# Two cross-attention layers: the order of the context loads, and the sources of one sum of adding transfers

## The chip, the core and the metric

The kernel runs on one core of one Trainium2 chip. The metric is the time of one execution in microseconds (us), as the device counts it; a kernel's time is the median of several executions. A profile is one more execution, and has its own time.

The engines are named as in the profile: PE is TensorE's matrix multiplication and PEld its loading of weights, DVE is VectorE, ACT ScalarE, POOL GpSimd, SP SyncE. SP computes nothing here; it issues transfers. A transfer is issued on the queue of the engine whose program holds it, and is carried by the core's 16 DMA engines.

## What is computed

Two layers of cross-attention over the same context `ctx` (8 batches of 1444 keys of width 512), for 8 batches of 100 queries of width 1024; all is float32. The reference, cut to what matters:

```python
def layer0(query, key):
    Q = query @ Wq + bq
    K = key @ Wk + bk
    V = key @ Wv + bv
    weights = softmax(Q @ K.T / sqrt(1024), axis=-1)
    return query + (weights @ V) @ Wo + bo

def layer1(emb, latent):
    q = emb @ Wq + bq
    k = latent @ Wk + bk
    v = latent @ Wv + bv
    w = softmax(q @ k.T / sqrt(1024), axis=-1)     # over the keys
    x = w @ v + emb
    return layernorm(x) * gamma + beta             # eps 1e-6

out = layer1(layer0(x, ctx), ctx)
```

## The kernel before

Keys and values are never formed. The kernel multiplies the weights first: `qk` is Wq Wk^T and `vo` is Wv Wo, so that the scores are (x `qk`) ctx^T and the result is (weights ctx) `vo`. All the large products of weights and of queries use a scheme with seven half products in place of eight (`weight_products`, L348; `queries`, L653; `inner_product`, L256). The stages follow each other on TensorE in the program's order, which is kept by hand for that engine (`manual_schedule(engines={PE})`, L64):

1. `qk` of layer 0, then `vo`, then the queries of layer 0, then `qk` of layer 1 (call at L846);
2. the scores of batches 0 and 1 of layer 0 (L1296 and L1299);
3. a loop over the eight batches (L1300). In each, `alternated` (L1284) interleaves the weighted rows of batch b (`weighted_rows`, L883) with the scores of batch b + 2 (`scores_by_keys`, L922), step by step. In the first turn the first 12 steps of the scores go ahead;
4. the output projection and the queries of layer 1, and then the same for layer 1.

**The context is loaded twice for each batch and layer.** `load_features` (L855) loads the transposed context ctx^T as four feature tiles of 128 rows by 1444, two transfers each; the scores of a batch go through them in order, 46 records of TensorE a tile (23 matrix multiplications, each of which the profile shows as two). `load_rows` (L864) loads the context itself as four row tiles of three blocks of 128 keys, one transfer a block; the last tile has two blocks and a remainder in two transfers. In this document cT_b_k is feature tile k of batch b and c_b_q is row tile q.

**Where the tiles lie.** Row tiles, and the feature tiles 0 and 1, take a buffer of the pool `unit` (L72), of which there are ten; the units of `qk`, eight of them, come from the same pool, as do some temporaries. The feature tiles 2 and 3 take a buffer with the tag `prob` (`feature_block`, L84), of which there are three: prob0, prob1 and prob2. A load into a buffer waits until all that used it before is done.

**What sets the order.** Outside TensorE a scheduler places each instruction on its engine when the kernel is built; where it holds that a buffer comes free late, it puts other instructions first. `tc.keep_in_program_order(instruction)` takes an instruction out of this freedom against others of its kind on the same engine. An engine executes its list in order, and an instruction that waits holds up those behind it; this is true of SP's list of loads too.

**The bias sums.** Four sums over the eight units of a weight product, each unit scaled by one bias per row, are made beside the products. Those of width 1024 go through `transferred_sum` (L547). It scales a unit into a tile on ScalarE (`scaled_sum`, L576; activations at L579, in program order), and then adds the tiles in pairs, as a tree, with adding transfers issued by GpSimd (`transfer_added`, L573; the transfers are at L574): tile 0 takes tile 1, tile 2 takes 3, 4 takes 5, 6 takes 7; then 0 takes 2 and 4 takes 6; then 0 takes 4. For `qk` of layer 1 all eight tiles are scaled at once. Its tiles are, by number: two rows, one weight row, prob0, prob1, prob2, and two weight rows. The same three prob buffers carry, just before, part of the key bias of layer 0 (`key_bias_sums`, L624, call at L844), which ends in a transfer that adds prob0 to the tile `kb`; and just after, the feature tiles 2 and 3.

The finished sum is read by VectorE in `block_sums` (L586; the transpose at L592 and the reduction at L595), after the softmax of batch 0 (call at L1298). ScalarE also copies finished half products out of PSUM (`put`, L436 to L438), between and behind the scalings; TensorE accumulates further on such a bank only after its copy.

As built, SP's loads after those of the weights were not in the program's order: batch 0 in order, then the first half of cT_1_2, then cT_1_0, the second half of cT_1_2, cT_1_1, then the row tiles of batch 0 mixed with the first feature tiles of batch 2, and cT_1_3 after all of c_0.

Of the kernel before, what the change touches and what calls it, by code (L numbers as in the profile page):

```python
# [31 lines left out]
P = 128  # L32
HP = P // 2
B, T, E = 8, 100, 1024
S, L = 1444, 512
# [11 lines left out]
LAST = (MC - 1) * P  # L47
PAD = S - LAST + QD
# [5 lines left out]
def two_layer_cross_attention(ctx: ExitStack, tc: tile.TileContext, a: dict, out: bass.AP):  # L54
    nc = tc.nc
# [16 lines left out]
    def unit(name):  # L72
        return stream.tile([P, E + L], F32, tag="unit", name=name)

    def wide(name):
        return work.tile([P, LC, GT], F32, tag="AT", name=name, bufs=2)

    def row(name):
        return work.tile([P, E], F32, tag="row", name=name, bufs=3)

    def weight_rows(name):
        return work.tile([P, MC * T], F32, tag="wT", name=name, bufs=3)

    def feature_block(name):  # L84
        return work.tile([P, S], F32, tag="prob", name=name, bufs=3)
# [262 lines left out]
    def weight_products(name, left, right, l_width, r_width, scaled, between=None):  # L348
# [35 lines left out]
        def accumulate(side):  # L384
            for v, of in scaled:
                if of != side:
                    continue
                width = (l_width, r_width)[side]
                first = 0 if side == 0 else l_width
                srcs = [(units[h][:, first : first + width], cols[v][:, h : h + 1]) for h in range(EC)]  # L390
                if width == E:
                    accs[v] = transferred_sum(f"{name}_{v}", srcs, name)
                    continue
                acc = work.tile([P, L], F32, tag="half", name=f"{name}_{v}", bufs=1)
                accs[v] = acc
                if early:
                    tiles = [acc] + [t[:, i * L : (i + 1) * L] for t in prob for i in range(2)]
                    scaled_sum(tiles + [weight_rows(f"{name}_{v}_7")[:, :L]], srcs)
                    continue
                for h, (src, by) in enumerate(srcs):  # L400
                    if h == 0:
                        vector.tensor_scalar(acc, src, by, None, ALU.mult)
                    else:
                        vector.scalar_tensor_tensor(acc, src, by, acc, ALU.mult, ALU.add)
# [142 lines left out]
    def transferred_sum(name, srcs, of):  # L547

        n = EC if of == "qk1" else EC // 2
        tiles = [row(f"{name}_{n}") for n in range(2)] + [weight_rows(f"{name}_2")[:, :E]]
        tiles += [t[:, :E] for t in prob]
        if of != "qk0":
            tiles += [weight_rows(f"{name}_{n}")[:, :E] for n in range(6, 8)]
        scaled_sum(tiles[:n], srcs[:n])

        def second_half():
            t = tiles[n]  # L560
            if of != "qk0":
                scaled_sum(tiles[n:], srcs[n:])
            else:
                for i, (src, by) in enumerate(srcs[n:]):
                    if i == 0:
                        vector.tensor_scalar(t, src, by, None, ALU.mult)
                    else:
                        vector.scalar_tensor_tensor(t, src, by, t, ALU.mult, ALU.add)
            transfer_added(tiles[0], t)

        return tiles[0], second_half

    def transfer_added(to, t):  # L573
        nc.gpsimd.dma_start(out=to, in_=t, accum_op=ALU.add)  # L574

    def scaled_sum(tiles, srcs):  # L576

        for t, (src, by) in zip(tiles, srcs):
            tc.keep_in_program_order(nc.scalar.activation(t, src, AF.Copy, scale=by))  # L579
        k = 1  # L580
        while k < len(tiles):
            for i in range(0, len(tiles) - k, 2 * k):
                transfer_added(tiles[i], tiles[i + k])
            k *= 2
# [39 lines left out]
    def key_bias_sums(name, wqbk, tiles=()):  # L624

        acc = to = work.tile([P, B * T], F32, tag="kb", name=name, bufs=1)

        def steps():
            if tiles:
                scaled_sum(tiles, [(xT[:, k, :], wqbk[:, k : k + 1]) for k in range(EC)])
            for k in range(len(tiles), EC):
                if k == len(tiles):
                    vector.tensor_scalar(to, xT[:, k, :], wqbk[:, k : k + 1], None, ALU.mult)
                else:
                    vector.scalar_tensor_tensor(to, xT[:, k, :], wqbk[:, k : k + 1], to, ALU.mult, ALU.add)
                yield
            if tiles:  # L640
                transfer_added(to, tiles[0])

        return acc, steps()
# [178 lines left out]
    for g in range(B // G):  # L822
# [3 lines left out]
                out=xT[:, :, g * GT : (g + 1) * GT],  # L826
                in_=a["xT"].rearrange("(c p) t -> p c t", p=P)[:, :, g * GT : (g + 1) * GT],
# [7 lines left out]
    qk1 = weight_products(  # L835
        "qk1", "L1_xattn_WqT", "L1_xattn_WkT", E, L, (("L1_xattn_bk", 0), ("L1_xattn_bq", 1)), lambda: None
    )
# [6 lines left out]
    kb0, more = key_bias_sums("kb0", wqbk0[:, :EC], [t[:, : B * T] for t in prob])  # L844
# [7 lines left out]
        tc.keep_in_program_order(nc.scalar.activation(xT[:, e, :], xT[:, e, :], AF.Identity, bias=bias))  # L852


    def load_features(b):  # L855

        for k in range(LC):
            name = f"cT_{b}_{k}"
            t = feature_block(name) if k >= LC // 2 else unit(name)[:, :S]
            for part in (slice(0, LAST // 2), slice(LAST // 2, S)):  # L860
                nc.sync.dma_start(out=t[:, part], in_=a["ctxT"][b][k * P : (k + 1) * P, part])
            yield t

    def load_rows(b):  # L864

        src = a["ctx_512"][b]
        for q in range(NQ):
            t = unit(f"c_{b}_{q}").rearrange("p (c l) -> p c l", c=CQ)
            n = CQ - (q == NQ - 1)
            r0 = q * CQ * P  # L870
            for i in range(n):
                nc.sync.dma_start(out=t[:, i, :], in_=src[r0 + i * P : r0 + (i + 1) * P, :])
            if n < CQ:
                more = PAD - (S - LAST)
                nc.sync.dma_start(out=t[: S - LAST, n, :], in_=src[LAST:S, :])
                nc.sync.dma_start(out=t[S - LAST : PAD, n, :], in_=src[:more, :])
            yield t

    def keys(m):
# [400 lines left out]
    def first_scores(b, layer, softmax):  # L1280

        return scores_by_keys(batches[b], layer, *loaded(load_features(b)), softmax)

    def alternated(b, layer, softmax, dst, first=0):  # L1284

        nxt = b + 2 < B
        c, *cT = loaded(load_rows(b), *([load_features(b + 2)] if nxt else []))
        A = weighted_rows(batches[b], layer, c, dst)
        ahead = scores_by_keys(batches[b + 2], layer, *cT, softmax) if nxt else iter(())
        run(islice(ahead, first))  # L1290
        for _ in range(MC * LC):
            next(A)
            next(ahead, None)
            yield
# [33 lines left out]
    kb1, more = key_bias_sums("kb1", wqbk1)  # L1328
# [29 lines left out]
    for bs in SETS:  # L1358
        t = wide(f"A1T_{bs[0]}").rearrange("p c t -> p (c t)")[:, : LC * len(bs) * T]
        t = t.rearrange("p (c t) -> p c t", c=LC)  # L1360
# [42 lines left out]
```

## Time and profile before

| What | Value |
|---|---|
| median of 3 executions | 599.59 us (598.75 to 599.96) |
| the profiled execution, its own time | 601.1 us |
| its span, from the first to the last instruction | 599.0 us |
| mean granted clock of TensorE | 0.988 of full speed |
| PE busy | 580.7 us, 97% of the span, 7470 records |
| PEld busy | 503.6 us, 84% |
| DVE busy | 393.5 us, 66% |
| ACT and POOL busy | 133.6 and 133.1 us, 22% each |
| moved by the DMA | 142.95 MB, mean 239 GB/s |
| weighted rows, L891 | 3072 records, 232.5 us |
| scores, L934 | 1472 and 1472 records, 116.4 and 116.2 us |

The profile has several views. A group's row gives line, engine, operation and tiles, then busy time and the mean time of one. A row of the timeline gives the start (in us from the span's start), the length, and the instruction, and in brackets how long its engine sat idle before it and what ended that. A row of waits names who waited for whom, then the total, the number of times and the longest. The chain is the work that ended last, followed back from the last instruction. A table of stages gives each engine's busy time in a stretch of the span, and at its end TensorE's granted clock, the mean busy share of the DMA engines, and what they moved. Tile names are shown without numbers, so cT<-in_ctxT is a load of any feature tile and c<-in_ctx of any row tile; a load's line is L861 (features) or L872 (rows). SPq is SP's list of transfers.

### The profile page before, as it was taken

What the parts mean: (1) busy time and instruction counts of PE and PEld (TensorE: products, weight loads), DVE (VectorE), ACT (ScalarE), POOL (GpSimd) and SP (SyncE); (2) the same over time, 40 slices, a digit from 0 to 9 for tenths busy, and PEclk for the clock granted to TensorE, in tenths of its full rate; (3) what the DMA queues carried; (4) which work ended last, traced back from release to release, by engine and by line L of the source; (5) the groups of instructions that cost most, each with busy time, mean ns of one, the idle gap of its engine ahead of it and who ended that gap; (6) DMA issues with size and microseconds to landing.
All of it is one profiled execution on the core that took longest, in us unless ns stands there. A gap on an engine that the chain in (4) does not pass through costs nothing.

```text
span 599.0 us, 17465 instructions
## 1 busy us (share of the span) xinstructions
PE 580.7 (97%) x7470; PEld 503.6 (84%) x7470; DVE 393.5 (66%) x912; ACT 133.6 (22%) x349; POOL 133.1 (22%) x206
## 2 busy tenths in 40 slices
PE   9999999999999499999999999999999999999994
PEld 8887457688899499999997856687999999999992
DVE  1996689888675555774468486885533327663695
ACT  1322320424500102011200000112333303144313
POOL 3110110311210222042223001202931121341052
PEclk9999999999999799999999999999999999999998
DMA  8959999854778999999991004995899992497114
GB/s 275 308 89 349 296 245 310 202 99 97 149 178 263 374 373 370 360 346 358 358 303 54 2 0 143 398 361 188 312 344 361 356 348 94 131 328 258 55 30 82
DMA packets 65096, 142.95 MB, mean 239 GB/s; under 512 B 7548, under 2 KB 12924, under 8 KB 65020
## 3 DMA queue, kind: packets, MB, share of 16 engines
q1 hardware_dynamic: 56574, 117.80, 55.9%
q0 software_dynamic: 8048, 23.57, 18.6%
q8 instruction: 59, 0.97, 0.6%
q10 hardware_dynamic: 398, 0.47, 0.2%
q14 instruction: 17, 0.14, 0.1%
HBM read 121.53 MB, written 6.14 MB: 213 GB/s over the span
## 4 chain that ended last, share of the span: by engine, by line
PE 73%; DMA 9%; issue 4%; POOL 1%; DVE 1%; ACT 1%; SPq 1%; POOLq 0%; DVEq 0%; ACTq 0%
PE A L891 21%; PE s L934 20%; PE o_x L164 5%; PE g_x L164 4%; PE qk_x L164 3%; PE o_y L164 3%; PE g_y L164 3%; DMA g_t<-xT 2%; DMA vo_L_xattn_bv<-vo_L_xattn_bv 2%; DMA cT<-in_ctxT 2%; PE o_w L164 1%; PE o_z L164 1%; PE qk_y L164 1%; PE qk_z L164 1%; DMA c<-in_ctx 1%
## 5 line engine op out<-in xcount | busy, mean ns | idle before, releaser
L891 PE MATMUL A<-w,c 128*64 128x100 f32 (+1 forms) x3072 | 232.5, 250 | 1.3 <-issue 1.3
L891 PEld LDWEIGHTS A<-w,c 128*64 128x64 f32 (+1 forms) x3072 | 205.2, 136 | 3.8 <-issue 3.5
L934 PE MATMUL s<-g0T,cT 128*64 128x100 f32 (+1 forms) x1472 | 116.4, 255 | 8.4 <-DMA cT<-in_ctxT 8.0
L934 PE MATMUL s<-g1T,cT 128*64 128x100 f32 (+1 forms) x1472 | 116.2, 249 | 0.0
L934 PEld LDWEIGHTS s<-g0T,cT 128*64 128x64 f32 (+1 forms) x1472 | 102.2, 139 | 9.3 <-DMA cT<-in_ctxT 8.2
L934 PEld LDWEIGHTS s<-g1T,cT 128*64 128x64 f32 (+1 forms) x1472 | 100.5, 135 | 1.9 <-issue 0.6
L1135 POOL TENSOR_TENSOR part<-w 128x500 f32<-128x500 f32 x16 | 24.5, 1529 | 138.3 <-ACT w L988 64.3
L1115 ACT ACTIVATE w<-w,negmax 128x100 f32<-128x100 f32 x96 | 35.2, 370 | 68.2 <-DVE negmax L97 68.2
L97 DVE TENSOR_REDUCE most<-s 128x100 f32<-128x400 f32 (+1 forms) x24 | 12.5, 525 | 44.7 <-PE s L934 44.5
L988 ACT ACTIVATE w<-w 128x400 f32<-128x400 f32 (+2 forms) x32 | 12.0, 444 | 132.3 <-DVE w L97 115.4
L97 DVE SCALAR_TENSOR_TENSOR w<-s,kb 128x400 f32<-128x400 f32 (+2 forms) x32 | 13.8, 462 | 42.0 <-PE s L934 41.8
L164 PE MATMUL qk_x<-qk 128*128 128x256 f32 x128 | 29.7, 380 | 0.0
L164 PEld LDWEIGHTS qk_x<-qk 128*128 128x128 f32 x128 | 23.3, 190 | 3.0 <-ACT qk L438 0.2
L946 POOL MEMSET w<- 68x100 f32 x16 | 3.8, 238 | 72.9 <-PE A L891 41.5
L1195 DVE SCALAR_TENSOR_TENSOR z<-vectors,r,z 100x512 f32<-100x512 f32 x16 | 11.4, 744 | 12.5 <-PE z L1193 12.4
L97 DVE TENSOR_TENSOR w<-w,rtotal 128x400 f32<-128x400 f32 (+2 forms) x32 | 18.8, 587 | 1.1
L1115 ACT ACTIVATION_READ_ACCUMULATOR w<-w,negmax 128x1 f32 x96 | 18.4, 191 | 0.0
L1208 ACT ACTIVATE z<-z,rstd 100x1024 f32<-100x1024 f32 x7 | 8.1, 1151 | 45.4 <-POOL rstd L1206 45.4
L97 DVE TENSOR_TENSOR xT<-xT,o_x 128x400 f32<-128x400 f32 (+1 forms) x32 | 15.9, 540 | 2.7 <-PE o_x L164 2.4
L669 ACT ACTIVATE g1T<-g_x,k 128x400 f32<-128x400 f32 x4 | 2.4, 596 | 60.2 <-PE g_x L164 60.0
L164 PE MATMUL vo_x<-vo 128*128 128x512 f32 x32 | 15.3, 595 | 0.0
L164 PE MATMUL qk_y<-qk_s 128*128 128x256 f32 x64 | 14.1, 379 | 0.0
(432 smaller groups left out, 1037.9 us busy)
## 6 DMA issues: line engine op xcount, KB each, us to landing
c<-in_ctx SPq DMA_DIRECT2D x176, 256.0 KB, 5.5
cT<-in_ctxT SPq DMA_DIRECT2D x64, 370.0 KB, 6.5
cT<-in_ctxT SPq DMA_DIRECT2D x64, 352.0 KB, 6.1
vo<-in_L_xattn_Wo SPq DMA_DIRECT2D x8, 512.0 KB, 8.7
qk<-in_L_xattn_WqT SPq DMA_DIRECT2D x8, 512.0 KB, 6.2
qk<-in_L_xattn_WqT SPq DMA_DIRECT2D x15, 256.0 KB, 4.9
xT<-in_xT SPq DMA_DIRECT2D x2, 1600.0 KB, 24.3
out<-vectors POOLq DMA_DIRECT2D x7, 400.0 KB, 10.4
```

What stands on the lines that cost most here:

```text
L97: ins = getattr(nc.vector, op)(*args, **kw)
L164: nc.tensor.matmul(banks[n // per][:, n % per * width : (n % per + 1) * width], lhs[i][:, n * P : (n + 1) * P], rhs[i], start=(fresh and i ...
L669: nc.scalar.activation(dst[g][:, c, :], banks[j][:, :GT], AF.Identity, bias=u[:, c : c + 1])
L891: nc.tensor.matmul(ps[h * HP : (h + 1) * HP, k * T : (k + 1) * T], c[m // CQ][:r, m % CQ, k * P + h * HP : k * P + (h + 1) * HP], w[:r, m, :],
L934: nc.tensor.matmul(banks[m // GM][h * HP : h * HP + n, m % GM * T : (m % GM + 1) * T], cT[k][:, o : o + n], q[:, k, t0 : t0 + T], start=(k ...
L946: nc.gpsimd.memset(s["w"][:PAD, MC - 1, :], 0.0)
L988: nc.scalar.activation(rows, rows, AF.Exp)
L1115: nc.scalar.activation(rows[:, i, :], rows[:, i, :], AF.Exp, bias=negmax[:, i : i + 1], accum_out=total[:, i : i + 1])
L1135: add(part, w[:, 0:5, :], w[:, 5:10, :], ALU.add)
L1195: nc.vector.scalar_tensor_tensor(z[:, half], bv1[j][:T], s["r"], ps[:T, :], ALU.mult, ALU.add)
L1208: nc.scalar.activation(z, z, AF.Copy, scale=rstd)
```

## The change

Two things are changed. In `transferred_sum`, for `qk` of layer 1 alone, the eight tiles are put in another order, so that the three prob tiles take the numbers 1, 3 and 5. And each load of the context, features and rows, in both layers, is issued through `loaded_in_order`, which keeps these loads in the program's order on SP. What is loaded, into which kind of buffer, and how much at a time stays the same; so does what is added.

```diff
@@ -554,6 +554,8 @@ transferred_sum
         tiles += [t[:, :E] for t in prob]
         if of != "qk0":
             tiles += [weight_rows(f"{name}_{n}")[:, :E] for n in range(6, 8)]
+        if of == "qk1":
+            tiles = [tiles[i] for i in (0, 3, 1, 4, 2, 5, 6, 7)]
         scaled_sum(tiles[:n], srcs[:n])
@@ -852,13 +854,16 @@
+    def loaded_in_order(to, src):
+        tc.keep_in_program_order(nc.sync.dma_start(out=to, in_=src))
+
     def load_features(b):
...
             for part in (slice(0, LAST // 2), slice(LAST // 2, S)):
-                nc.sync.dma_start(out=t[:, part], in_=a["ctxT"][b][k * P : (k + 1) * P, part])
+                loaded_in_order(t[:, part], a["ctxT"][b][k * P : (k + 1) * P, part])
             yield t
@@ -869,11 +874,11 @@ load_rows
             for i in range(n):
-                nc.sync.dma_start(out=t[:, i, :], in_=src[r0 + i * P : r0 + (i + 1) * P, :])
+                loaded_in_order(t[:, i, :], src[r0 + i * P : r0 + (i + 1) * P, :])
             if n < CQ:
                 more = PAD - (S - LAST)
-                nc.sync.dma_start(out=t[: S - LAST, n, :], in_=src[LAST:S, :])
-                nc.sync.dma_start(out=t[S - LAST : PAD, n, :], in_=src[:more, :])
+                loaded_in_order(t[: S - LAST, n, :], src[LAST:S, :])
+                loaded_in_order(t[S - LAST : PAD, n, :], src[:more, :])
             yield t
```

## The prediction

> **What bounds the kernel now.** I read the busy shares first, then TensorE's waits, the timeline around the one long wait, the chain that ended last, and from there backwards the queues that feed it. TensorE is busy 97% of the span (580.7 of 599.0 us), so only its idle time, or time at a low clock, can be saved. TensorE's waits on the transposed context and its timeline:
>
> ```profile
> PE s L934 <- DMA cT<-in_ctxT: 8.0, 1, 8.0
> ...
> 184.06 14.63 PE L934 MATMUL s<-g0T,cT 128*64 128x100 f32 x322
> 206.73 6.92 PE L934 MATMUL s<-g0T,cT 128*64 128x100 f32 x91 [8.03 <-DMA cT<-in_ctxT]
> ```
>
> [...]A batch's scores are four feature tiles of 46 records. 322 is seven tiles: batch 0 whole, and three of batch 1. The fourth tile of batch 1 (cT_1_3, my name for feature tile 3 of batch 1) is 8.03 us late. The records after the wait take 6.92/91 = 76 ns each, those before it 14.63/322 = 45.4 ns. The stage table shows why (us; busy time of PE, PEld, DVE, ACT, POOL; then clock, DMA share, GB/s):
>
> ```profile
> 163.00:183.00 20.00, 20.00 (x148) 19.00 (x147) 15.36 (x43) 2.22 (x6) 2.83 (x6) 1.00 0.78 180
> 183.00:199.00 16.00, 15.70 (x326) 14.76 (x324) 10.07 (x26) 0.34 (x1) 0.00 (x0) 1.00 0.91 323
> 199.00:206.80 7.80, 0.07 (x2) 0.07 (x4) 3.10 (x6) 1.20 (x4) 3.70 (x7) 0.69 1.04 352
> 206.80:228.00 21.20, 21.20 (x425) 21.20 (x427) 11.72 (x29) 1.49 (x4) 3.74 (x7) 0.87 1.01 372
> 228.00:300.00 72.00, 71.25 (x1612) 70.65 (x1610) 41.85 (x115) 12.84 (x24) 18.51 (x33) 1.00 1.02 359
> ```
>
> The clock falls to 0.69 in the wait and is 0.87 on average in the 21 us after it: 0.13 x 21.2 = 2.8 us more. Why the tile is late, from the chain, and from SP's own waits:
>
> ```profile
> 186.06 1.48 SPq L861
> 187.65 0.42 SPq L872
> 188.11 6.53 DMA c<-in_ctx
> 194.66 6.32 DMA cT<-in_ctxT
> 201.03 5.65 DMA cT<-in_ctxT
> 206.73 6.92 PE s L934 x91
> ```
> ```profile
> SPq L861 <- DMA qk_L_xattn_bk<-prob: 23.5, 2, 17.4
> ```
>
> SP stood 17.4 us, to 183.79, at the first half of cT_1_2, whose tile is the buffer prob1 that the bias sum held to its last adding transfer. Then it issued the rest of batch 1, all of c_0 and two tiles of batch 2, and only then, at 201.03, cT_1_3. GpSimd's timeline shows the adding transfers that hold it:
>
> ```profile
> 156.36 0.86 POOL L574 DMA_DIRECT2D qk_L_xattn_bk<-prob  x1 [5.56 <-ACT prob L579]
> 158.44 0.86 POOL L574 DMA_DIRECT2D prob<-prob  x1 [1.23 <-ACT prob L579]
> ...
> 179.15 0.86 POOL L574 DMA_DIRECT2D qk_L_xattn_bk<-prob  x1 [3.78 <-DMA prob<-qk_L_xattn_bk]
> ```
>
> The first frees prob0, and SP's next load goes at 161.07; the second frees prob2 (next load at 164.11); the last, from 179.15, frees prob1 at 183.79.
>
> **What the Trainium skill says.** "TensorE: Matmul & The Clock Gate", section "What's actually happening": an idle window halves TensorE's clock, and some 3.4 us of work restore it. The trace agrees in kind: 76 against 45.4 ns after the wait. "DMA: Bandwidth & Descriptors", section "Anatomy of one DMA — SWDGE (gpsimd) path": the DMA engines wait on no semaphore, the issuing sequencer does. The trace agrees: for 17.4 us no load behind the waiting one was issued. Same page, "Queues, rings and completion order": each DMA engine takes turns between the queues. So the loads that now go earlier share with the adding transfers; no row of before shows the price, and I bound it below.
>
> **Part 1, the tree.** As built, the eight scalings of the second sum now write row, prob0, row, prob1, weight rows, prob2 and two weight rows. The first level adds prob0, prob1 and prob2 away: all three are sources, none a destination. Instruction count, sizes and the number of levels are unchanged: eight scalings, seven adding transfers.
> ScalarE: the second scaling now needs prob0, so ScalarE stops after one scaling where it stopped after three. The stop ends, as before, when the key bias transfer has landed, at 154.92. Before, five scalings followed it (3.23 + 2.17 us, to 160.2); now seven do, 7 x 1.08 = 7.6, to 162.5. Queued behind them are the copies of Y and X (L438), which before ran from 160.13 and 162.55: four at about 0.5 us put X's first copy at 164.1, where TensorE needs it at 164.27 (the first accumulation on X again). Cost 0 to 0.8; I take 0.2. VectorE's subtraction in place on the fourth unit, about 159.0, needs that unit's scaling, done at 154.9 + 3.2 = 158.1: hidden.
> GpSimd: prob0's transfer goes at about 156.4 (free at 161.1, as before), prob1's at 158.6 (free about 164), prob2's at 160.7 (166 to 168). No level's end gets earlier: the last transfer must wait for ScalarE's later end and lands at 185 to 190 by my count. VectorE wants that sum at 200.9 (the transpose at L592): 10 us of cover, hidden. GpSimd clears three weight rows between these transfers, the third now after the last landing; its first weight sum ran at 201.14: hidden too. The key bias transfer now goes ahead of the sum's first adding transfer, not beside it, and may land a little earlier: a gain I leave at nothing.
>
> **Part 2, the loads in program order.** TensorE's, VectorE's (until batch 6) and ScalarE's other orders are the same as built. SP's first loads become: all of batch 0, all of batch 1, then c_0, cT_2 and so on in turns.
> cT_1_0 and cT_1_1 need the units 0 and 1 of the weight product, last read near 166.9 and 170.4 (the product's groups of four records at 166.03 and 169.54). So they and cT_1_2 go at 167 to 172, not after 183.79. cT_1_3 takes prob0 again, and waits for the third tile of batch 0: 184.06 + 138 x 0.0454 = 190.3. Behind it stand all c_0 and cT_2; c_0 went from 187.65 before. That is the added wait.
> Who needs what: cT_1_3 lands at 190.3 + 0.8 (two issues) + 5.65 = 196.8 at worst; TensorE wants it at 198.7 (184.06 + 14.63). Batch 1 ends at 200.8. Then cT_2_0 is wanted at 200.8, c_0_0 and cT_2_1 at 202.9, and a further pair each 4.2 us. A feature tile is 0.74 MB, a row tile 0.79. The DMA moved 376 GB/s from 190 to 206 us (the same table for that stretch). At this rate the 7.4 MB issued from 183.79 on take 19.7 us, and the last landed 22.9 us after the start: 3.2 us for issue and first landing. So from 193.5: cT_2_0 at 193.5 + 2.26/0.376 = 199.5, c_0_0 earlier, cT_2_1's first half at 193.5 + 3.41/0.376 = 202.6, cT_2_2's at 206.6 for 207.1, c_1_0 and cT_3_0 at 193.5 + 8.24/0.376 = 215.4 for 217.3. In time, the narrowest by 0.3 us; at 359 GB/s 0.1 us late. Cost 0 to 0.5; I take 0.1. The weights of batch 0 are ready at 200.2 (ScalarE's row at 198.66, 1.54 long).
> Afterwards a batch takes TensorE (380 records x 44.7 ns) 17.0 us, and its 5.9 MB take 16.5 us at 359 GB/s: the loads keep their lead.
> Is the DMA drained by 190? From 158 to 173.75 the engines were 99% busy and moved 3.52 MB, 1.48 of it two feature tiles: the rest took about 3 us per adding transfer. Seven of these and five tiles (2 us each) are 31 us of DMA time from 156.4: to 187.5. Barely. If not drained, up to 4 us late.
> The second layer gets the same order: cT_1_3 there waits for the third tile of its batch 0 (406.4) and holds c_0, which went at 380.9 before. TensorE wants c_0_0 and cT_2_0 at 423.9; 2.26 MB after 406.4 + 3.2 land at 415.6: 8 us of cover. In its later batches a row tile waits for a unit that comes free some 12 us before the data is wanted, and a feature tile stands behind it: hidden.
> VectorE: the first two query sums (1.43 + 1.23 us) and one subtraction (1.23) move from batch 5 to around batch 6's end, ahead of the additions that free the banks; these end 2.7 us later, 1.2 of it won before. The spare bank is wanted at 330.8 and free about then: 0.1 to 0.5 us; I take 0.1.
>
> **Sum.** Wait 8.03, low clock 91 x (76 - 45.4) ns = 2.8, less 0.2, 0.1 and 0.1: 10.4 us. The profiled execution took 601.1 (span 599.0 and 2.1 around it): 590.7. The median of the runs, 599.59, lies 1.5 below it: 589.2.
>
> **Rivals.**
> *A shorter wait comes back* at c_0_0 or cT_2_1, from the DMA still busy with adding transfers: 1.5 to 4 us of wait, and with the longest of these the clock falls again (2.8). For it: 187.5 against 190.3. Against: the adding transfers thin out towards their end (two waits for a landing in a row), and c_0_0 itself has 4 us of cover. Time 589.2 + 1.5 to 589.2 + 6.8: 590.7 to 596. Chance 0.2.
> *The wait only moves* and stays about 8 us long (the load at the head of SP's queue is freed when TensorE is already at its end): within 1.2 us of 599.6. Against: cT_1_3 goes at 190.3, 8.4 us ahead of need. Chance 0.03.
> *Slower: the queue's head blocks in each batch.* Between 193.5 and the last tile pair of batch 5, 36.3 MB must land (cT_1_3, six batches of rows and six of features). Before, this pair was wanted at 306.6 (batch 5's rows end at 312.9, L910's records, and the pair starts 6.3 earlier). If waiting heads pull the mean below 36.3/(306.6 - 193.5) = 321 GB/s, the kernel loses; at 300 the pair lands at 314.5, 7.9 us later: 607.5. Against: before ran at 359 with SP waiting for freed buffers part of that time, and ten units leave a lead. Chance 0.07.
>
> **How the numbers follow.** Forecast 0.70: 588 to 590.6. Range 587.6 to 594.0: the floor is the whole 10.8 and the 0.8 us by which the fastest run lay below the median, with 0.4 more for a key bias transfer that lands earlier; the ceiling takes more than half of the first rival. Left out is about 0.18. A measurement tells 0.2% (1.2 us) from no change: faster 0.90, same 0.03, slower 0.07.
>
> **What would show it.** After: no wait of TensorE on the context near 199, records of batch 1's last tile at 45 ns, the clock at 1.00 from 183 to 228, SP's cT issues at 167 to 172 and then a gap to 190.3, batch 0's weighted rows ending near 217.3 (228.2 before), and everything later 10 to 11 us earlier. Wrong if a wait on c or cT of over 1 us stands between 199 and 217, if ScalarE's late copies stop TensorE at 164, or if waits on loads appear after 400.

## The result, and the profile after

| | before | after |
|---|---|---|
| median | 600.06 us (598.57 to 603.18, 20 executions) | 597.77 us (593.22 to 600.22, 20 executions) |
| ratio | 1 | 0.9954, 95% interval 0.9935 to 0.9973 |
| profiled execution | 601.1, span 599.0 | 599.5, span 597.6 |
| granted clock, mean | 0.988 | 0.994 |

The ratio, here and below, is formed from the fast executions alone and need not be the quotient of the two medians. Faster by 0.46%, where 1.7% was forecast: 597.8 us, not 589.2, and outside the range. Lines of the code lie a little lower now: the scores are L939 (before L934), the weighted rows L896 (L891), all context loads L858, the adding transfers L576 (L574).

The step that the change was made for did what was forecast. TensorE's timeline after, and SP's:

```profile
184.00 1.51 PE L652 MATMUL kb<-kb,ones 128*128 128x400 f32 x4
185.44 18.67 PE L939 MATMUL s<-g0T,cT 128*64 128x100 f32 x413
203.86 0.30 PE L896 MATMUL A<-w,c 128*64 128x100 f32 x1
```
```profile
191.86 0.80 SPq L858 DMA_DIRECT2D cT<-in_ctxT  x2
192.76 1.33 SPq L858 DMA_DIRECT2D c<-in_ctx  x3
194.19 0.85 SPq L858 DMA_DIRECT2D cT<-in_ctxT  x2
```

The 322 and the 91 records of before are one row of 413, 18.67/413 = 45.2 ns each, with no wait in it: the fourth tile of batch 1 is in time. It was issued at 191.86, ahead of all of c_0, where before it was issued at 201.03. The stages show the clock at full speed:

```profile
183.00:199.00 16.00, 16.00 (x320) 15.14 (x320) 10.13 (x25) 0.00 (x0) 1.23 (x3) 1.00 0.62 176
199.00:206.80 7.80, 7.80 (x177) 7.69 (x175) 7.60 (x15) 1.49 (x4) 3.74 (x7) 1.00 1.05 402
206.80:228.00 21.20, 20.13 (x448) 19.49 (x444) 14.20 (x39) 4.64 (x10) 5.48 (x10) 1.00 1.04 367
425.00:491.00 66.00, 63.94 (x1397) 63.02 (x1394) 21.29 (x62) 15.31 (x76) 17.09 (x36) 1.00 1.02 358
```

Read the second number of a row against the first: TensorE's busy time against the stretch. The first two rows are full. The last two are not: 1.07 and 2.06 us are missing, at full clock. So the loss sits in places where nothing was lost before. TensorE's waits after name them:

```profile
PE s L939 <- issue: 2.6, 6, 0.9
PE o_z_x L164 <- DVE xT L97: 1.9, 1, 1.9
PE A L896 <- issue: 1.7, 4, 0.6
```

Against the one long wait of before stand one wait for VectorE and ten short ones put down to "issue": no releaser is known. The page of before had 1.3 and 0.3 us of these in four waits. No wait on a load is left.

**Where the time went, record by record.** TensorE runs the same 7470 records in both profiles, in the order that the program sets, so the start of each can be compared:

| where | after minus before |
|---|---|
| from 15 us to the end of the weight products | +1.2 to +1.4 us |
| past batch 1's last tile | -9.3 (a gain of 10.7; forecast 10.8 ahead of costs) |
| 206 to 222 us | to -7.6 |
| 222 to 320 us | to -8.1 (before has short waits of its own here) |
| 320 to 328 us | -8.1 to -4.6 |
| 425 to 490 us | to -2.3 |
| end, after one more short wait at 540 us | -1.4 |

The first row is no part of the change: TensorE's clock was first granted at full at 4.1 us in the profile of before and at 6.5 in that of after; 2.5 us at half clock is 1.2 us.

**The wait for VectorE.** TensorE's timeline after:

```profile
319.94 0.50 PE L164 MATMUL o_z_x<-A0T,vo 128*128 128x200 f32 x2
320.27 0.50 PE L164 MATMUL o_z_z<-A0T,vo 128*128 128x200 f32 x2
320.61 0.50 PE L164 MATMUL o_z_y<-o_t,o_t 128*128 128x200 f32 x2
323.02 0.61 PE L164 MATMUL o_z_x<-o_t,o_t 128*128 128x200 f32 x2 [1.91 <-DVE xT L97]
325.10 5.09 PE L896 MATMUL A<-w,c 128*64 128x100 f32 x88
```

The inner product writes the bank o_z_x and accumulates into it again three small products later, once VectorE has added the first part into xT. VectorE's timeline after shows what stood ahead of that addition:

```profile
315.56 0.28 DVE L97 TENSOR_TENSOR o_t<-vo,o_t 128x128 f32<-128x128 f32 x1
315.76 1.21 DVE L97 TENSOR_TENSOR g_s<-qk 128x1024 f32<-128x1024 f32 x1
...
317.59 1.57 DVE L97 TENSOR_TENSOR g_s<-g_s,qk 128x1024 f32<-128x1024 f32 x1
319.08 0.56 DVE L925 TENSOR_TENSOR A0T<-A,rrow 128x400 f32<-128x400 f32 x1
319.56 1.04 DVE L97 TENSOR_TENSOR xT<-xT,o_x 128x400 f32<-128x400 f32 x2
320.52 1.21 DVE L97 TENSOR_TENSOR qk<-qk 128x1024 f32<-128x1024 f32 x1
321.66 1.04 DVE L97 TENSOR_TENSOR xT<-xT,o_z 128x400 f32<-128x400 f32 x2
322.62 0.35 DVE L97 TENSOR_TENSOR xT<-xT,o_z_x 128x200 f32<-128x200 f32 x1
```

The same views of before, VectorE and then TensorE:

```profile
308.93 1.43 DVE L97 TENSOR_TENSOR g_s<-qk 128x1024 f32<-128x1024 f32 x1 [4.28 <-PE A L891]
...
323.90 0.28 DVE L97 TENSOR_TENSOR o_t<-vo,o_t 128x128 f32<-128x128 f32 x1
...
328.74 0.36 DVE L97 TENSOR_TENSOR xT<-xT,o_z_x 128x200 f32<-128x200 f32 x1
```
```profile
329.15 0.61 PE L164 MATMUL o_z_x<-o_t,o_t 128*128 128x200 f32 x2
```

Before, the query sums ran in idle time 15 us earlier, and the addition ended at 329.10 for a use at 329.15: a slack of 0.05 us at most. After, VectorE reached the last sum o_t 8.34 us earlier but the addition only 6.12 us earlier. The 2.2 us between had no slack to go into. The clock then stood at one half for 3.4 us (323.97 to 327.38 us in the trace's record of the clock): the 88 records after the wait take 5.09/88 = 57.8 ns each, not 45. Together this is the step of 3.5 us at 320 to 328.

That is the profiled execution. The twenty executions of the changed kernel differ in their mean granted clock. Six had 0.993 or 0.994 and took 597.2 to 600.2 us; four had 0.998 and took 593.2 to 595.8. In the 36 executions of the six kernels below whose profile has no wait for VectorE here, none had less than 0.995. So the half clock after this wait most likely comes in some executions and not in others. The record has no trace of a spared one.

### The profile page after: what moved, and what is told of

It reads as the page before. It is cut to its first block, busy times and chain, and to the rows that moved or that the text cites. A ratio compares the mean times of both kernels' runs of the same rounds, so it can differ in the third digit from the quotient of the medians.

```text
span 597.6 us, 17446 instructions
## 1 busy us (share of the span) xinstructions
PE 582.5 (97%) x7470; PEld 503.4 (84%) x7470; DVE 393.2 (66%) x912; ACT 133.7 (22%) x349; POOL 136.1 (23%) x206
## 4 chain that ended last, share of the span: by engine, by line
PE 94%; issue 2%; POOL 1%; DVE 1%; ACT 1%; DVEq 0%; POOLq 0%
PE s L939 22%; PE A L896 22%; PE qk_x L164 7%; PE g_x L164 5%; PE o_x L164 5%; PE vo_x L164 3%; PE o_y L164 3%; PE g_y L164 3%; PE qk_y L164 2%; PE qk_z L164 2%; PE o_z L164 1%; PE o_w L164 1%; PE qk_w L164 1%; PE vo_y L164 1%; PE vo_z L164 1%
## 5 line engine op out<-in xcount | busy, mean ns | idle before, releaser
L896 PE MATMUL A<-w,c 128*64 128x100 f32 (+1 forms) x3072 | 234.0, 251 | 1.9 <-issue 1.7
L896 PEld LDWEIGHTS A<-w,c 128*64 128x64 f32 (+1 forms) x3072 | 203.1, 137 | 4.4 <-issue 3.9
L939 PE MATMUL s<-g1T,cT 128*64 128x100 f32 (+1 forms) x1472 | 116.4, 250 | 1.8 <-issue 1.8
L939 PE MATMUL s<-g0T,cT 128*64 128x100 f32 (+1 forms) x1472 | 114.1, 250 | 0.8 <-issue 0.8
L939 PEld LDWEIGHTS s<-g1T,cT 128*64 128x64 f32 (+1 forms) x1472 | 99.9, 135 | 4.2 <-issue 3.5
L939 PEld LDWEIGHTS s<-g0T,cT 128*64 128x64 f32 (+1 forms) x1472 | 96.9, 135 | 2.8 <-issue 2.1
L576 POOL DMA_DIRECT2D qk_L_xattn_bk<-qk_L_xattn_bk x6 | 5.2, 922 | 45.5 <-ACT qk_L_xattn_bk L581 17.7
```

The costliest lines, as they stand in the source:

```text
L896: nc.tensor.matmul(ps[h * HP : (h + 1) * HP, k * T : (k + 1) * T], c[m // CQ][:r, m % CQ, k * P + h * HP : k * P + (h + 1) * HP], w[:r, m, :],
L939: nc.tensor.matmul(banks[m // GM][h * HP : h * HP + n, m % GM * T : (m % GM + 1) * T], cT[k][:, o : o + n], q[:, k, t0 : t0 + T], start=(k ...
```

## The experiments

**Each part alone.** The tree alone takes the changed kernel and gives back the scheduler its loads; the loads alone take it without the new tree.

```diff
 tree alone:   def loaded_in_order(to, src):
-        tc.keep_in_program_order(nc.sync.dma_start(out=to, in_=src))
+        nc.sync.dma_start(out=to, in_=src)
 loads alone:
-        if of == "qk1":
-            tiles = [tiles[i] for i in (0, 3, 1, 4, 2, 5, 6, 7)]
```

Expected of the tree alone: 

> The new tree, with the loads left to the scheduler as before: SP's order and VectorE's order are the ones of the kernel before. Theory (the tree alone frees the buffer that blocked SP, and what was lost later comes from the moved VectorE work): the wait of 8.03 us and the 2.8 us of low clock are gone or nearly so, the query sums stay in idle VectorE time, no wait at the accumulation on o_z_x near 323: about 10 us faster than before, 590 us against 600. Rival 1 (the order of the loads does the work): cT_1_3 still stands behind c_0 to c_3 and two tiles of batch 2 on SP, a wait of 3 to 8 us on it stays, 594 to 600. Rival 2 (saturated DMA gives the gain back): as after, about 598.

Expected of the loads alone: 

> The loads in program order, with the tree as before: cT_1_2 waits to about 184 for the bias sum's last adding transfer, cT_1_3 goes at 190.3 as in the changed kernel, and SP's and VectorE's orders are those of the changed kernel. Theory (from 190 on the changed kernel's queue is set by cT_1_3, not by the tree): cT_1_2 lands by 190 for 196, so the same time as the changed kernel, 597 to 598, with the same wait of about 1.9 us at o_z_x. Rival (both parts are needed): the batch 1 features come late, a wait of 2 us or more on cT near 195 to 199, 600 or more.

Measured: the tree alone 591.9 us, ratio to before 0.9871 (0.9846 to 0.9897). The loads alone 597.87, ratio 0.9967 (0.9948 to 0.9986), which is the changed kernel again. The tree alone has these waits:

```profile
PE s L939 <- DMA cT<-in_ctxT: 1.0, 1, 1.0
PE s L939 <- issue: 0.9, 2, 0.7
PE A L896 <- issue: 0.7, 1, 0.7
```

and the loads alone these:

```profile
PE s L939 <- issue: 3.5, 6, 0.9
PE A L896 <- issue: 2.3, 6, 0.7
PE o_z_x L164 <- DVE xT L97: 2.1, 1, 2.1
```

Either part alone removes all of the old wait but 1 us at most. With the tree, SP is no longer stopped to 183.8: c_0 goes at 174.6, not 187.65, and what stands ahead of cT_1_3 is nearly through when its buffer comes free. With the order, cT_1_3 stands ahead of them. The parts do the same job twice. The rival that only the order does the work falls, and so does the one that both parts are needed. With the order comes what the changed kernel lost: both kernels that have it show the moved VectorE work and the wait at o_z_x, and the tree alone has neither.

**The VectorE order mended.** In the changed kernel, the additions of the last product's first part and the query sums are both kept in the program's order, so that the sums follow the additions.

```diff
         if b == B - 2:
+            vector.in_order = True
             for part in parts:
                 run(part)
+            vector.in_order = False
...
                 if n in (7, 11, 15):
+                    vector.in_order = True
                     next(queries1)
+                    vector.in_order = False
```

> The changed kernel with VectorE's order fixed: the additions into xT of the last product's first part stay ahead of the two query sums and the subtraction (1.21, 1.57 and 1.21 us), which come after them. Theory (these three instructions delay the addition that frees the bank): the 1.9 us wait at o_z_x near 323 and the 3.4 us at half clock after it (1.7 us) go: 3.5 us faster than the changed kernel, 594. Rival (the loss is TensorE's own supply of instructions, or noise): within 1 us of the changed kernel, 597 to 598.

Measured: 593.61 us, ratio 0.9893 (0.9863 to 0.9923), clear of the changed kernel's interval (0.9935 to 0.9973); 0.61% or 3.7 us by the ratios. The expected 594 holds. The rival, a time within 1 us of the changed kernel, falls. TensorE's timeline there:

```profile
317.90 0.50 PE L164 MATMUL o_z_y<-o_t,o_t 128*128 128x200 f32 x2
318.32 0.61 PE L164 MATMUL o_z_x<-o_t,o_t 128*128 128x200 f32 x2
```

The wait is gone (the new part starts at 318.32, when the addition, from 317.91, is done), and no half clock follows it. The cause holds; how the 3.7 us divide is less sure, since this profile has by chance none of the changed kernel's 1.6 us of short waits in the first layer (table below).

**The second layer's loads.** The changed kernel with the order kept in the first layer only; and the tree alone with the order kept in the second layer only. In each pair SP's list in the second layer is all that differs. The diff is of the first; the other has the two values the other way round.

```diff
+    keep_loads = [tc.keep_in_program_order]
     def loaded_in_order(to, src):
-        tc.keep_in_program_order(nc.sync.dma_start(out=to, in_=src))
+        keep_loads[0](nc.sync.dma_start(out=to, in_=src))
...
+    keep_loads[0] = lambda ins: ins
     scores1 = first_scores(0, 1, softmax1)
```

First layer only: 

> The changed kernel with the loads in program order in the first layer only; in the second the scheduler places them. TensorE, VectorE, ScalarE and GpSimd have the changed kernel's orders. Theory (in-order loads of the second layer crowd the DMA just when TensorE's next block of instructions is fetched): the five short waits without a releaser at 425 to 541 (2.7 us together, 0.34 in the kernel before) shrink to below 1 us, 595.5. Rival (such waits fall by chance, in any order of the loads): as many of them, 597 to 598.

Second layer only: 

> The tree, with the loads in program order in the second layer alone. TensorE, VectorE, ScalarE and GpSimd have the orders of the tree alone, and SP has until the second layer. Theory (in-order loads of the second layer cost TensorE short waits for its own instructions): 591.9 + 3.0 = 594.9, with 2 to 3 us of short waits without a releaser after 425 (0.7 in the tree alone). Rival (such waits fall by chance): 591.5 to 592.5.

Measured: first layer only 594.78 us, ratio 0.9932 (0.9907 to 0.9958); second layer only 594.09, ratio 0.9894 (0.9864 to 0.9924). By the ratios the order in the second layer costs 1.3 us in one pair and 1.4 in the other, less than expected, and the intervals overlap: the times alone leave it open. The waits do not. With the order in the first layer only:

```profile
PE A L896 <- issue: 1.5, 2, 1.0
PE o_z_x L164 <- DVE xT L97: 1.2, 1, 1.2
```

and in the second only:

```profile
PE s L939 <- issue: 1.9, 4, 0.7
PE A L896 <- issue: 1.6, 3, 0.7
PE s L939 <- DMA cT<-in_ctxT: 0.5, 1, 0.5
```

With the order in the first layer only, no short wait is left after 425; with it in the second only, there are five of over 0.2 us. The first kernel's wait for VectorE is 0.7 us shorter than the changed kernel's. For 0.5 of it the trace has a reason: a short wait at 304 us held TensorE back while VectorE, busy without a pause from 302.7 us to the addition, went on. This profile was the fastest of its kernel's eleven executions (591.28 us, the median 594.78).

**What the short waits are.** The profile gives them no releaser. The list of DMA queues holds a candidate, here of the kernel after:

```profile
q8 instruction: 59, 0.97, 0.7%
```

That is 59 packets of 16.4 KB; if they are TensorE's, with 7470 multiplications and as many weight loads, it is one packet for some 127 records. "Runtime: NRT & Kernel Launch", section "Instruction fetch mechanics", of the Trainium skill says that an engine's instructions are fetched in blocks of 16 KiB through a DMA queue while it works, and calls the cost mostly hidden. The size agrees. In the trace, all 52 waits over 0.2 us that carry no releaser, in ten profiles, end 2.3 to 2.8 us after the start of such a packet, while the packets themselves come about every 6 us. And they fall at the same records of TensorE's list, one block or a few apart:

```
kernel                  number of the record after the wait (wait, ns), 206 to 222 us and from 425 us
after                   1341 (526) 1469 (249) 1595 (296) | 4641 (262) 4767 (872) 5775 (279) 5901 (643) 6786 (682)
loads alone             1341 (664) 1469 (249) 1595 (311) | 4767 (538) 4892 (914) 5522 (450) 6786 (896)
additions first         none                             | 5144 (512) 5269 (339) 5901 (657) 6786 (957)
order in second layer   1341 (414)                       | 4892 (365) 5144 (725) 5396 (709) 5522 (510) 6786 (682)
```

The neighbours are 125 to 128 records apart, which is no tile's length. Record 1341 shows best what decides. In three kernels the packet ahead of it starts while TensorE is at record 1263, 1280 or 1281, and there is no wait. In the other seven it starts at records 1296 to 1309, and TensorE waits 0.16 to 0.96 us, by and large longer the later the packet. The packet starts before the wait, so the wait does not bring it about. These are, by all of this, TensorE's own instructions, late.

**Fewer loads.** To ask whether the loads make them late, the kernel with the additions first and all loads in order was run with less to load, in the second layer and then in both. It leaves out two of three row blocks in most row tiles, so its results are not those of the two layers. The diff is of both; for one, the condition asks for the layer as well.

```diff
-            for i in range(n):
+            for i in range(1 if thin and q < NQ - 1 else n):
                 loaded_in_order(t[:, i, :], src[r0 + i * P : r0 + (i + 1) * P, :])
...
-                        c[m // CQ][:r, m % CQ, k * P + h * HP : k * P + (h + 1) * HP],
+                        c[m // CQ][:r, 0 if m // CQ < NQ - 1 else m % CQ, k * P + h * HP : k * P + (h + 1) * HP],
```

Second layer: 

> The changed kernel with the additions ahead of the query sums, all loads in program order, and in the second layer two of three row blocks of each of the first three row tiles of a batch are left out: the products read the first block three times, so TensorE's instructions and their sizes stay and 1.5 of a batch's 5.9 MB are not moved. Theory (the short waits without a releaser are TensorE's instruction blocks, fetched late by DMA engines that are kept full): none of more than 0.2 us after 425, where the kernel with all loads has four with 2.5 us together; 593.6 - 2.9 = 590.7. Rival (they come from something in TensorE's own stream, not from the DMA): the same four waits, 593 to 594.

Both layers: 

> As the kernel with fewer loads in the second layer, but in both layers: two of three row blocks of each of the first three row tiles of every batch are left out and the first block is read three times; all loads in program order, the additions ahead of the query sums, TensorE's instructions and their sizes unchanged. Theory (what is left between the two corrections and the forecast is TensorE's late instruction blocks in the first layer): no wait without a releaser over 0.2 us after 200 but perhaps one, no wait on loads, 588.5 to 589.5, the forecast number. Rival (that rest has another cause): as with the second layer's loads thinned alone, 591 to 592.

Measured: 591.25 us, ratio 0.9845 (0.9815 to 0.9875), for the second layer; 588.84, ratio 0.9817 (0.9784 to 0.985), for both. Waits with the second layer thinned, and then with both:

```profile
PE A L896 <- issue: 3.4, 6, 0.9
PE s L939 <- issue: 0.4, 1, 0.4
```
```profile
PE A L896 <- issue: 0.5, 1, 0.5
```

All six of the first row lie in the first layer, which is loaded in full there; after 425 only the 0.4 is left (2.5 us with all loads). With both thinned one wait remains, at 208 us, where the profile still counts the DMA as 102% busy (199 to 228 us). The stage from 425 to 491 us with all loads, with the second layer thinned and with both thinned:

```profile
425.00:491.00 66.00, 64.49 (x1295) 63.57 (x1291) 26.09 (x71) 18.31 (x92) 12.06 (x25) 1.00 0.96 336
425.00:491.00 66.00, 65.61 (x1377) 65.26 (x1374) 25.04 (x68) 16.95 (x85) 15.31 (x32) 1.00 0.78 259
425.00:491.00 66.00, 66.00 (x1306) 65.85 (x1302) 27.62 (x74) 19.87 (x100) 12.05 (x25) 1.00 0.74 243
```

TensorE's instructions are the same in number and size in all three, so the rival that the cause lies in TensorE's own stream falls for the second layer: with room on the DMA the blocks arrive in time. A full DMA alone does not make a block late, though. All 52 packets ahead of a wait started after 3 us in which the DMA was at least 93% busy; but so busy (over 90%) it was ahead of 373 packets from 200 to 545 us in the ten profiles, and 321 of these were in time. The times support the thinning less firmly than the waits: the intervals of "additions first", "second layer thinned" and "both layers thinned" overlap, each with the next. All ten kernels, waits of over 0.2 us without a releaser (us), in one execution each:

| kernel | first layer | second layer | second layer's loads |
|---|---|---|---|
| before | 1.2 | 0.3 | scheduler |
| tree alone | 0.9 | 0.7 | scheduler |
| order in first layer only | 1.5 | 0.0 | scheduler |
| both corrections (below) | 0.7 | 1.3 | scheduler |
| after | 1.6 | 2.7 | in order |
| loads alone | 2.8 | 2.8 | in order |
| additions first | 0.0 | 2.5 | in order |
| order in second layer only | 0.4 | 3.0 | in order |
| second layer thinned | 3.4 | 0.4 | in order, fewer |
| both layers thinned | 0.5 | 0.0 | in order, fewer |

In the second layer the two kinds of list, loaded in full, don't overlap: 0 to 1.3 against 2.5 to 3.0. The profiled execution was not always a typical one: those of "tree alone" and "order in first layer only" were the fastest of their kernels, those of "after" and "loads alone" 1.7 and 3.0 us above their medians. Without these four, 0.3 and 1.3 still stand against 2.5 and 3.0. In the first layer the waits vary from 0.0 (additions first) to 3.4 (second layer thinned) with the same list of loads, so there it is largely chance, and the 0.5 of the last row shows nothing for the first layer.

**Both corrections.** The order in the first layer only, and the additions first (both diffs above together).

> The changed kernel with both corrections: loads in program order in the first layer only, and the additions into xT ahead of the query sums. Theory (the two losses are separate and add up: 4.2 us by the fixed VectorE order, 3.0 us by the scheduler's loads in the second layer): 597.8 - 7.2 = 590.6, a little under the tree alone (591.9), since no wait of about 1 us on cT_1_3 is left; no wait at o_z_x, at most one short wait without a releaser after 425. Rival (the losses overlap): 593 to 594, no better than the better of the two alone.

Measured: 592.25 us, ratio 0.9855 (0.983 to 0.9879). Faster than before and than the changed kernel, beyond the intervals; by the ratios 5.9 us under the changed kernel where 7.2 was expected. That the two losses add up is likely but not shown: the interval overlaps that of the additions first alone (0.9863 to 0.9923). It can't be told from the tree alone (0.9871), which needs only the two lines of the tree. These two are the best complete versions found.

## Why the prediction was wrong

**What bounds the kernel** was read rightly. In the profiles the opening gained 10.7 us where the working had 8.03 + 2.8; the trees and loads behaved as worked out: cT_1_0 issued at 168.3 and cT_1_2 at 173.5 (167 to 172 forecast), cT_1_3 at 191.9 (190.3), the first copy of X at 163.93 (164.1), the last adding transfer landed at 191.5 (185 to 190) and stopped nobody. No load was late for TensorE. None of the prediction's three signs of being wrong occurred: they looked at loads and at ScalarE, and the losses came by other ways.

**The step that failed is the one on VectorE**, "the spare bank is wanted at 330.8 and free about then: 0.1 to 0.5 us; I take 0.1". In the profile it cost about 3.6 us: 1.91 of wait and 1.7 at half clock; without the delay the kernel is 3.7 us faster by the ratios. That the sums would move ahead of the additions was forecast, and the delay itself was not far off (2.7 us less 1.2 won before, 1.5, forecast; 2.2 measured). What was wrong is the consumer: the prediction looked at the spare bank that the weighted rows take next, and not at the bank o_z_x, on which the same inner product accumulates again 1.6 us earlier, and where the page of before showed a slack of 0.05 us. And the price of a stall's low clock, which the prediction set for the wait that goes and for its first rival, it did not set here.

**A term was missing: TensorE's own instructions.** The prediction asked of each load whether it would be in time, and priced a hold in the second layer at nothing ("8 us of cover"). The loads were in time. But TensorE's blocks of instructions, carried by the same DMA, came late five times there. Measured: 2.7 us of waits against 0.3 in the profiles; 1.3, 1.4 and, from "additions first" to "both corrections", 2.3 us by the ratios, three pairs that point one way, though the intervals of each pair overlap. Before and after, from 365 to 425 us, and before from 425 on:

```profile
365.00:425.00 60.00, 60.00 (x550) 45.36 (x550) 43.33 (x83) 10.54 (x39) 15.77 (x19) 1.00 0.82 303
365.00:425.00 60.00, 60.00 (x634) 46.46 (x633) 43.95 (x85) 14.22 (x58) 17.45 (x20) 1.00 0.71 247
425.00:491.00 66.00, 65.66 (x1487) 65.20 (x1483) 23.19 (x63) 18.76 (x97) 21.66 (x41) 1.00 0.99 345
```

With the hold the DMA moved 247 GB/s ahead of 425 us, not 303, and had more to move afterwards. But from 425 to 491 us it was as good as full before too (0.99, after 1.02). Why lists in order make the blocks later there stays open; when a block was asked for is not in the trace.

**A term was read from one execution.** The 2.8 us of low clock come from a profile with a mean granted clock of 0.988. Of the 54 executions of the kernel before that ran beside the experiments, 47 had 0.990 or more, with a median of 0.991. That is some 3.6 us less at half clock (0.003 x 599 us, twice), so for the median execution the term may have been up to 1.8 us too large. This is an estimate: how much of that time was work is not on record.

**A question was not asked:** what is each part worth alone? The sum priced both together. The tree alone would have been cheaper to predict: VectorE's order is then as before.

**The account.** In ratios to before, times 600 us: changed kernel to additions first 3.7 us; to the second layer thinned 2.9; to both thinned 1.7. Together 8.2 us, and the forecast was missed by 0.9954 - 589.2/599.59 = 0.0127, which is 7.6. With the additions first and room on the DMA the kernel takes 588.84 us, close to the forecast number. In part that is luck: with a quarter of the context's bytes left out it also lacks most of the 1.5 us of short waits that the kernel before had, a gain that the forecast did not count. Of the three steps only the first is clear of the intervals.

**The rivals.** A wait coming back on c_0_0 or cT_2_1 did not occur; the losses were of other kinds, and the time lies above the range of that rival (590.7 to 596). The wait did not stay, and the loads kept their pace in each batch. Faster by over 0.2% was right.

## What to carry to other kernels

If two edits aim at one wait, price each alone: the second may add nothing but its side effects. When instructions move on an engine that is not the bound, check every consumer of what they delay, the nearest first, and read its slack off the trace: 0.05 us of slack is a wait of the full delay, and its low clock may come on top. A full DMA also carries the instructions of the engine that bounds the kernel, and here one block in seven came late in such stretches (52 of 373).

## What was not expected of the hardware

- TensorE stops for its own instructions: up to 0.96 us at a time, 5.6 us in one profile (loads alone), at boundaries of some 127 records, each time after 3 us in which the DMA was 93% busy or more.
- Waits of 1.91 and 2.08 us were followed by 3.4 us at half clock; waits of 1.17 us and less were not. "TensorE: Matmul & The Clock Gate", section "What's actually happening", gives some 3.4 us for both the idle window and the recovery. The recovery agrees; idle of 1.9 us was enough here, and after the 8.03 us wait of before the half clock lasted 10.2 us in all, 5.5 of them after the wait.
- In each of the ten traces the full clock lasts for whole multiples of 3.413 us (580.27 us is 170 of them, 317.44 is 93), and so does each half clock in mid-kernel. If the clock is set once in such a step, it matters where in the step a wait falls; that was not tested.
- The first grant of the full clock came between 4.1 and 6.7 us in the ten profiles, which by an estimate (2.6 us at half clock) makes up to 1.3 us of difference between two executions of the same work.
